# One stream over sequences, layers and groups in a fused scan, attention and feed-forward kernel

## The chip, the cores and the metric

The kernel runs on one core of a Trainium2 chip. The metric is the device time of one execution in microseconds; for each version the median of its runs is given. A profile is one further execution under the hardware profiler; its span is about 2 us shorter than the time of that execution.

## The reference

The input `x` is 32 sequences of 256 tokens with 256 features, float32. A first part is a small state-space model; two layers of local attention and feed-forward follow; the input is added at the end.

```
# scan part, per sequence
xr, gate = split(x @ W_in.T);  xr += cond
xc = silu(causal_conv4(xr));   xn = layernorm(xc)
B, C, dt = split(xn @ W_xproj.T);  dt = 0.01*tanh(dt @ W_dt.T + b_dt)
h = clip(h * (1 + dt*A) + B*min(|xn|,1) * xn[t], -10, 10)   # 256 steps, 16 states x 512
y = (C . h + D*xn) * silu(gate) @ W_out.T
# two layers, x = y
q, k, v = split(shift(x) @ wqkv);  q, k = l2norm, scale, rotary
x = x + local_attention(q, k, v, window 128, 8 heads of 64) @ wo
a, g = split(layernorm(shift(x)) @ w1 + b1)                  # 2 x 682
x = x + (a * gelu(g)) @ w2 + b2
# out = input + x
```

`shift` moves half of the features on by one token.

## The kernel before, in words

The sequences form four groups of eight (`NG = 4`, `GB = 8`). The program is recorded once; the order in which the recording calls are made sets, apart from small moves, the order of the instructions on each engine.

**Setup.** All constants are loaded on the ScalarE queue and prepared ahead of everything: the folded weights `wx_sb`, `wsum`, `wbias`, the rotary tables, the head tables. One flag, `bounded`, decides by a branch between two forms of the softmax; everything below is inside the branch that runs.

**Scan.** `group_scan` treats a group's eight sequences together in 8 chunks of 32 tokens. It keeps an agenda: each piece of work has a slot, slot t being the one in which step t is done. A chunk is prepared 43 to 4 slots before its first step: `project` (PE), convolution (DVE, GpSimd, ScalarE), norm, a transposition through DRAM. Each step is one custom VectorE instruction (`step`, L576) on a row `xrep` that was spread over the states by a DMA (512 KB for two rows, three buffers) and scaled by ScalarE (`scale_row`, L569). In the first group half of the rows are spread by TensorE instead (`by_tensor`). Read-out (`y`, L588), gate and output projection follow; the last piece is in slot 271. Result: `ys` in DRAM.

**Layers.** The group's residual is kept in SBUF in four tiles `res0` to `res3` of two sequences. In `Attention`, `project` makes q, k and v of half a sequence (L786) and rotates q and k on DVE and GpSimd; `turn` transposes them (L825); `scores`, `sums`, `values`, `divide` and `finish` (L836) do the rest. In `FeedForward`, two sequences go together: `normalise`, `spread`, then six chunks of `widen` (L1116, 512 columns), a Gelu and a product, and `narrow` (L1145), which adds up in two PSUM banks over all six. All PSUM tiles come from one pool of eight banks.

**Order.** The scan of group 0 runs alone. Then for each group `blocks` yields slot by slot: eight sequences of attention, eight slots each, then feed-forward of four pairs, and the same for layer 1. `side_by_side` lets the scan of the next group advance in even shares of its 316 pieces beside these slots, and ends it before the last pair. So attention and feed-forward are phases of a layer; each scan starts only when the last one has ended; the last group runs with no scan beside it. Weights of a layer come in four loads (`wqkv`, `wo`, `w1`, `w2`), each into one buffer.

Of the kernel before, what the change touches and what calls it, by code (L numbers as in the profile page):

```python
# [73 lines left out]
def kernel(  # L74
# [46 lines left out]

    w_in_sb = loaded(w_inT, [P, KM, 2 * DI], "w_in_sb", nc.sync)
# [5 lines left out]
    dskip_sb = loaded(d_skip.partition_broadcast(P), [P, DI], "dskip_sb")  # L128
    w_out_sb = loaded(w_outT, [P, NC_, DM], "w_out_sb")
    flg_sb = loaded(f_ln_g, [P, L, KM], "flg_sb")  # L130
    flb_sb = loaded(f_ln_b, [P, L, KM], "flb_sb")
    b1_sb = loaded(b1, [P, L, 2, len(MCH)], "b1_sb")
    b2_sb = loaded(b2, [P, L, KM], "b2_sb")
# [34 lines left out]
    nc.scalar.activation(a_sb, a_sb, AF.Tanh)  # L168
    nc.vector.tensor_scalar(a_sb, a_sb, -1.0, 0.01, ALU.mult, ALU.mult)


    nc.vector.tensor_scalar(w_out_sb, w_out_sb, 0.5, None, ALU.mult)


# [20 lines left out]
    for h in range(HEADS):  # L195
        row = 32 * (h // 2) + 16 * (h % 2)
        nc.vector.tensor_copy(
            head_rows[:, h, :], ident[:, row : row + 1].broadcast_to([P, DH])
        )

    b1g_sb = const.tile([P, L], FP, tag="b1g_sb", name="b1g_sb")
    nc.scalar.dma_start(
        out=b1g_sb[DH : DH + MREM], in_=b1[0:MREM, :, 1, len(MCH) - 1]
    )

    bounded = const.tile([1, 1], I32, tag="bounded", name="bounded")

# [8 lines left out]
    with tc.tile_pool(name="setup", bufs=2) as setup, tc.tile_pool(  # L216
        name="setup_ps", bufs=2, space=PSUM
    ) as sps:

        for src, pos, dst in ((qk_scale, rot_c, rc_sb), (qk_scale_sw, rot_s, rs_sb)):  # L220
            tab = setup.tile([P, NW, 2, DH], FP, tag="tab", name="tab")
            nc.scalar.dma_start(out=tab, in_=pos)
            for l in range(L):
                sc = setup.tile([P, 2 * DH], FP, tag="qk_sc", name="qk_sc")
                nc.scalar.dma_start(
                    out=sc, in_=src[l].rearrange("a d -> (a d)").partition_broadcast(P)
                )
                for w in range(NW):
                    nc.vector.tensor_mul(
                        dst[:, l, w].rearrange("p a d -> p (a d)"),  # L230
                        tab[:, w].rearrange("p a d -> p (a d)"),
                        sc,
                    )

        sq = setup.tile([1, L, 2, DH], FP, tag="sq", name="sq")
        nc.scalar.dma_start(out=sq, in_=qk_scale.unsqueeze(0))
        nc.vector.tensor_mul(sq, sq, sq)
        big = setup.tile([1, L, 2], FP, tag="big", name="big")
        nc.vector.tensor_reduce(big, sq, AX.X, ALU.max)
        nc.vector.tensor_mul(big[:, :, 0], big[:, :, 0], big[:, :, 1])  # L240
        nc.vector.tensor_scalar(big[:, :, 1], big[:, :, 0], SCALES2, None, ALU.is_le)
        allb = setup.tile([1, 1], FP, tag="allb", name="allb")
        nc.vector.tensor_reduce(allb, big[:, :, 1], AX.X, ALU.min)
        nc.vector.tensor_copy(bounded, allb)

        wx0 = setup.tile([P, NC_, 3 * NS], FP, tag="wx0", name="wx0")
        nc.scalar.dma_start(out=wx0, in_=w_xT)
        wdt_sb = setup.tile([NS, NS], FP, tag="wdt", name="wdt_sb")
        nc.scalar.dma_start(out=wdt_sb, in_=w_dtT)
        gcol = setup.tile([P, NC_], FP, tag="gcol", name="gcol")  # L250
        nc.scalar.dma_start(out=gcol, in_=s_ln_g.rearrange("(c p) -> p c", p=P))

        cols = setup.tile([P, NC_, 2], FP, tag="cols", name="cols")
        nc.gpsimd.memset(cols[:, :, 0:1], 1.0)
        nc.scalar.dma_start(out=cols[:, :, 1], in_=s_ln_b.rearrange("(c p) -> p c", p=P))
        for c in range(NC_):
            td = sps.tile([P, P], FP, tag="td", name="td")
            nc.tensor.transpose(td[0:NS, :], wx0[:, c, 2 * NS : 3 * NS], ident)
            wdT = setup.tile([NS, P], FP, tag="wdT", name="wdT")
            nc.vector.tensor_copy(wdT, td[0:NS, :])  # L260
            td2 = sps.tile([P, P], FP, tag="td", name="td2")
            nc.tensor.matmul(td2[:, 0:NS], wdT, wdt_sb, start=True, stop=True)
            nc.vector.tensor_copy(wx0[:, c, 2 * NS : 3 * NS], td2[:, 0:NS])
        nc.gpsimd.memset(wx_sb, 0.0)
        nc.vector.tensor_mul(wx_sb[:, :, 0 : 3 * NS], wx0, bc(gcol, 2, 3 * NS))
        for i in range(3):
            for src, k, dst in ((wx_sb, 0, wsum), (wx0, 1, wbias)):
                wide = setup.tile([P, NC_, NS, GB], FP, tag="wide", name="wide")
                nc.vector.tensor_copy(wide, bc(src[:, :, i * NS : (i + 1) * NS], 3, GB))
                tw = sps.tile([P, 2], FP, tag="tw", name="tw")  # L270
                for c in range(NC_):
                    nc.tensor.matmul(
                        tw,
                        wide[:, c].rearrange("p n b -> p (n b)"),
                        cols[:, c, :],
                        start=(c == 0),
                        stop=(c == NC_ - 1),
                    )
                nc.vector.tensor_copy(dst[:, i : i + 1], tw[:, k : k + 1])
        nc.vector.tensor_add(wbias[:, 2:3], wbias[:, 2:3], bdt_sb)  # L280
# [9 lines left out]
    def program(ctx, exact):  # L290
# [13 lines left out]

        def reorder(out, ps):

            nc.scalar.copy(
                out.rearrange("p (q i b) -> p b i q", q=NQ, b=GB),
                ps.rearrange("p (b i q) -> p b i q", q=NQ, b=GB),
            )  # L310

        def group_scan(g, ys):
# [9 lines left out]
            agenda = {}  # L322
# [3 lines left out]
            def at(s, what, *args):  # L326
                agenda.setdefault(s, []).append(partial(what, *args))
# [357 lines left out]
            def put_y(c, d):  # L685
                nc.scalar.dma_start(
                    out=ys[:, d, :, c * CH : (c + 1) * CH], in_=ck[c].pop(("yo", d))
                )

            def start():  # L690
                h0 = hp.tile([P, DI], FP, tag="h", name="h0")
                nc.vector.memset(h0, 0.0)
                state["h"] = h0

# [10 lines left out]
            if alone:  # L705
                at(-30, spread_weights)
            for c in range(NCH):
                for t in range(CH):
                    at(c * CH + t, step, c, t)
            for c in range(NCH):  # L710
                s0 = c * CH

# [27 lines left out]
                for d in range(KM):  # L740
                    at(s0 + 44 + 2 * d, copy_y, c, d)
                    at(s0 + 45 + 2 * d, put_y, c, d)
            for c in range(NCH):
# [23 lines left out]
            for s in range(min(agenda), max(agenda) + 1):  # L767
                for what in agenda.get(s, ()):
                    what()
                yield  # L770

        SCAN_PIECES = NCH * CH + 44 + 16

        def load_res(ys, j):
            t = rpool.tile([P, KM, 2, 1 + S], FP, tag=f"res{j}", name=f"res{j}")
            nc.gpsimd.memset(t[:, :, :, 0:1], 0.0)
            for k in range(KM):
                nc.sync.dma_start(out=t[:, k, :, 1:], in_=ys[:, k, 2 * j : 2 * j + 2, :])
            return t

        def project_qkv(l, res, wqkv_sb, b, w, a):
            ps = bank(ps_w, "w", "ps_qkv")
            for k in range(KM):
# [4 lines left out]
                    res[b // 2][:, k, b % 2, t0 : t0 + W],  # L788
                    wqkv_sb[:, k, a * DI : (a + 1) * DI],
# [42 lines left out]
        def project_out(res, wo_sb, b, oT):  # L832
            po = ps_w.tile([P, KM, S], FP, tag="w", name="ps_wo")
            for d in range(KM):
                for c in range(NC_):
                    nc.tensor.matmul(  # L836
                        po[:, d],
                        wo_sb[:, c, d * P : (d + 1) * P],
# [4 lines left out]
            rv = res[b // 2][:, :, b % 2, 1:]  # L843
# [15 lines left out]
        def attention(l, res, wqkv_sb, wo_sb):  # L859

            for b in range(GB):

                qTs, kTs, vs = [], [], []
                for w in range(NW):
                    for a in (2, 0, 1):
                        ps = project_qkv(l, res, wqkv_sb, b, w, a)
# [14 lines left out]
                oT = ap_.tile([P, NC_, S], FP, tag="oT", name="oT")  # L881
# [66 lines left out]
                project_out(res, wo_sb, b, oT)  # L948
                yield

        class Attention:
# [3 lines left out]
            def __init__(self, l, res, wqkv_sb, wo_sb):  # L955
                self.l, self.res, self.wqkv, self.wo = l, res, wqkv_sb, wo_sb
                self.qkv, self.rot, self.p, self.o = {}, {}, {}, {}

            def project(self, b, w, a):
                if w == 0 and a == 2:  # L960
                    self.qkv[b] = [
                        ap_.tile([P, HEADS // 2, S], FP, tag=n, name=n) for n in ("qT", "kT")
                    ] + [ap_.tile([P, NW, DI], FP, tag="v", name="v_sb")]
                ps = project_qkv(self.l, self.res, self.wqkv, b, w, a)
# [56 lines left out]
            def values(self, b):  # L1021
                oT = ap_.tile([P, NC_, S], FP, tag="oT", name="oT")
# [34 lines left out]
        class FeedForward:  # L1057
# [80 lines left out]
            def narrow(self, j, m):  # L1138
# [13 lines left out]
                if m < len(MCH) - 1:  # L1152
                    return
# [287 lines left out]
```

## Time and profile before

Three runs: 4162.62 us in the median (4139.63 to 4162.65). The profiled run has a span of 4150.5 us at a mean granted TensorE clock of 0.959.

| engine | busy us | share of the span | instructions |
|---|---|---|---|
| PE (matmul) | 3797.3 | 91% | 18236 |
| PEld (weight load) | 2008.9 | 48% | 18236 |
| DVE | 2627.6 | 63% | 4986 |
| ACT | 1810.9 | 44% | 3345 |
| POOL | 1699.9 | 41% | 1749 |

A float32 matmul shows as two records. Matmuls are pipelined and the end of a record is modelled, so PE counts as busy while it waits a little; periods between starts tell more. The timeline gives these landmarks: the first projection of the scan at 37.3 us, the first step at 69.6 us, the first projection of q, k and v at 478 us, the last step of the last scan at 3364 us, the end at 4150 us. The group of DVE steps is 894.7 us for 1024 steps (874 ns each), the scaling of rows on ScalarE 609.4 us for 896, with 702.6 us of idle time before them that ended with the DMA of the row.

### The profile page before, as it was taken

Reading aid. Unit: us, or ns where it says so; the run is one execution under the profiler, and the core shown is the slowest. Engines: PE = TensorE matmul, PEld = TensorE weight load, DVE = VectorE, ACT = ScalarE, POOL = GpSimd, SP = SyncE. Lnnn points to the kernel's source line nnn. Section 1 sums busy time; section 2 is a strip of 40 time slices with the busy share of each in tenths; the row PEclk is TensorE's granted clock in tenths of the full one; section 3 lists DMA queues with packets and bytes.
Section 4 is the critical chain, followed back from the end, with each engine's and each line's share of the span. In section 5 each row is a group of like instructions: output and inputs, shape, how many; then the busy total and the mean of one; then the engine's idle time right before and its main releaser. Section 6 shows DMA issues by size and latency. Waiting matters only on the chain. (4 is left out here: it accounts for less than half of the span.)

```text
span 4150.5 us, 51929 instructions
## 1 busy us (share of the span) xinstructions
PE 3797.3 (91%) x18236; PEld 2008.9 (48%) x18236; DVE 2627.6 (63%) x4986; ACT 1810.9 (44%) x3345; POOL 1699.9 (41%) x1749
## 2 busy tenths in 40 slices
PE   5898898899989999899898999889998899999999
PEld 3333355544555455444455445554455545654653
DVE  5888567777766456767767636777776744434433
ACT  2655344545445334444544424454544533323331
POOL 3333265325543166423654136532554316513531
PEclk8988899999999999999999999999999999999999
DMA  4444312444335312444433421244433421000000
GB/s 118 123 113 113 80 44 72 128 120 119 92 84 146 81 44 76 114 111 120 106 88 113 124 65 44 75 127 119 119 90 91 139 77 37 8 14 22 1 11 32
DMA packets 257346, 353.10 MB, mean 85 GB/s; under 512 B 160867, under 2 KB 170420, under 8 KB 254900
## 3 DMA queue, kind: packets, MB, share of 16 engines
q1 hardware_dynamic: 172624, 337.67, 29.8%
q10 hardware_dynamic: 84452, 12.01, 1.9%
q8 instruction: 147, 2.41, 0.3%
q14 instruction: 123, 1.01, 0.1%
HBM read 314.49 MB, written 33.55 MB: 84 GB/s over the span
## 5 line engine op out<-in xcount | busy, mean ns | idle before, releaser
L576 DVE CUSTOM_DVE_ANT_0 h<-h,xrep,lim 128x512 f32<-128x512 f32 x1024 | 894.7, 874 | 82.5 <-PE y L588 23.3
L569 ACT ACTIVATE xrep<-xrep,beta 128x512 f32<-128x512 f32 x896 | 609.4, 716 | 771.2 <-DMA xrep<-xnd 702.6
L786 PE MATMUL ps_qkv<-wqkv_sb,res 128*128 128x512 f32 x1536 | 750.2, 628 | 32.5 <-ACT oT L1036 8.2
L810 POOL TENSOR_TENSOR rot<-rot,swp 128x512 f32<-128x512 f32 x256 | 327.4, 1279 | 655.1 <-DVE swp L807 597.8
L786 PEld LDWEIGHTS ps_qkv<-wqkv_sb,res 128*128 128x128 f32 x1536 | 290.5, 199 | 386.9 <-issue 304.9
L818 POOL TENSOR_TENSOR rn<-ss,neg_half 128x8 f32<-128x8 f32 x256 | 436.7, 1706 | 23.3 <-DVE ss L816 11.7
L802 DVE TENSOR_TENSOR rot<-ps_qkv,rc_sb 128x512 f32<-128x512 f32 x256 | 175.7, 686 | 393.3 <-ACT sq L799 392.9
L1145 PE MATMUL po_f<-ag,w_sb 128*128 128x512 f32 (+1 forms) x768 | 358.9, 618 | 21.6 <-DVE ag L1126 21.5
L588 PE MATMUL y<-h,ly 128*32 128x512 f32 x2048 | 362.0, 631 | 14.3 <-DVE h L576 13.1
L1116 PE MATMUL pa<-hT,w_sb 128*128 128x512 f32 (+1 forms) x896 | 364.0, 597 | 0.0
L1126 DVE SCALAR_TENSOR_TENSOR ag<-pa,b_sb,gl 128x512 f32<-128x512 f32 x192 | 143.5, 748 | 320.3 <-PE pa L1116 147.5
L1116 PE MATMUL pg<-hT,w_sb 128*128 128x512 f32 x640 | 309.8, 607 | 0.3 <-ACT gl L1124 0.3
L333 PE MATMUL ps_in<-xg,w_in_sb 128*128 128x256 f32 x1024 | 291.1, 414 | 12.8 <-issue 4.5
L819 POOL TENSOR_TENSOR rot<-rot,rn 128x512 f32<-128x512 f32 x256 | 280.1, 1094 | 19.0
L380 DVE SCALAR_TENSOR_TENSOR acc<-xr,wc_sb,acc 128x256 f32<-128x256 f32 x384 | 199.4, 523 | 111.1 <-POOL acc L369 108.5
L1079 POOL TENSOR_TENSOR rstd<-ve,neg_half 128x1 f32<-128x1 f32 x128 | 77.9, 609 | 467.3 <-DVE ve L1077 461.6
L333 PEld LDWEIGHTS ps_in<-xg,w_in_sb 128*128 128x128 f32 x1024 | 191.0, 201 | 156.0 <-issue 71.9
L1000 ACT ACTIVATE pT<-sc 128x512 f32<-128x512 f32 x384 | 206.1, 592 | 127.4 <-PE sc L991 114.0
L836 PE MATMUL ps_wo<-oT,wo_sb 128*128 128x256 f32 x1024 | 237.3, 385 | 0.0
L1145 PEld LDWEIGHTS po_f<-ag,w_sb 128*128 128x128 f32 (+1 forms) x768 | 135.4, 191 | 203.1 <-issue 133.5
L799 ACT ACTIVATE sq<-ps_qkv 128x512 f32<-128x512 f32 x256 | 148.1, 592 | 187.0 <-PE ps_qkv L786 141.5
L991 PE MATMUL sc<-qT,kT 64*128 64x128 f32 (+1 forms) x2048 | 227.1, 352 | 1.9 <-ACT kT L830 1.8
(152 smaller groups left out, 5615.2 us busy)
## 6 DMA issues: line engine op xcount, KB each, us to landing
xrep<-xnd SPq DMA_DIRECT2D x448, 512.0 KB
xnd<-xn SPq DMA_DIRECT2D x64, 256.0 KB
wqkv_sb<-in_wqkv_dram SPq DMA_DIRECT2D x8, 1536.0 KB
xd<-xnd SPq DMA_DIRECT2D x192, 64.0 KB
w_sb<-in_w_dram SPq DMA_DIRECT2D x8, 1364.0 KB
xg<-in_xT_dram SPq DMA_DIRECT2D x64, 128.0 KB
ys<-yo ACTq DMA_DIRECT2D x64, 128.0 KB
res<-ys SPq DMA_DIRECT2D x32, 256.0 KB
```

Source lines behind the costliest of these rows:

```text
L333: nc.tensor.matmul(ps, w_in_sb[:, k, ch * P : (ch + 1) * P], ck[c]["xg"][:, k], start=(k == 0), stop=(k == KM - 1),)
L569: nc.scalar.activation(bx, ck[c].pop(("bx", t), bx), AF.Copy, scale=ck[c]["beta"][:, t : t + 1])
L576: nc.vector._custom_dve(TENSOR_ADD_SAT, out=h_new, in0=state["h"], in1=bx, s0=ck[c]["lim"][:, 0, t : t + 1], s1=ck[c]["lim"][:, 1, t : t + 1],
L588: nc.tensor.matmul(ck[c]["y", hb][32 * q : 32 * q + 32, :], ly[hb % 2][:, 32 * t : 32 * t + 32], ck[c].pop(("h", hb * TB + t)), start=(i = ...
L786: nc.tensor.matmul(ps, res[b // 2][:, k, b % 2, t0 : t0 + W], wqkv_sb[:, k, a * DI : (a + 1) * DI], start=(k == 0), stop=(k == KM - 1),)
L810: nc.gpsimd.tensor_add(rot, rot, swp)
L818: nc.gpsimd.tensor_tensor(rn, ss, neg_half, ALU.pow)
L819: nc.gpsimd.tensor_mul(rot, rot, bc(rn, 2, DH))
L836: nc.tensor.matmul(po[:, d], wo_sb[:, c, d * P : (d + 1) * P], oT[:, c, :], start=(c == 0), stop=(c == NC_ - 1),)
L991: nc.tensor.matmul(banks[r][:, i, :], kT[rows, i0 + i, kw * W : (kw + 1) * W], qT[rows, i0 + i, kw * W :], start=False, stop=(i == n - 1),)
L1116: nc.tensor.matmul(ps[0:n, :], self.w1[:, k, half_ * HID + o : half_ * HID + o + n], self.h[j][:, k].rearrange("p b t -> p (b t)"), start= ...
L1145: nc.tensor.matmul(self.po[d], self.w2[r0 : r0 + n, m, d * P : (d + 1) * P], self.ag[m][r0 : r0 + n, :], start=(m == 0), stop=(m == len(MC ...
```

## The change

The layers become one stream of 64 sequences (4 groups x 2 layers x 8), each with eight slots (`ST = 8`). In the slots of sequence n stand the attention of n, the projections of n + 1, `divide`, `finish` and `normalise` of n - 1, `spread` and `widen` of n - 2, and `narrow` of n - 3, over layers and groups without a break. It is meant to give TensorE other work where one sequence's attention waits, and to spread the load of the other engines evenly. For it

- feed-forward handles one sequence at a time: 256 columns for 512, Gelu and its product in one tile `ag`, one PSUM bank for both halves of `widen` and one for `narrow`, which runs all six chunks in a row;
- the residual has a tile for each sequence, weights come in slices (three of `qkv`, six of `w1`), each fetched when the last reader of the old one is past;
- qT, kT and oT have one buffer each, not two;
- the scans of all groups share one agenda: group g + 1 starts 256 slots after group g, so its preparation and first steps run beside the end of the one before. `scan_to` paces it: to slot 273 before the layers, then evenly to slot 529 in the first 114 slots of the stream, then 256 scan slots for 128;
- `bounded` is worked out first, from one load, and the rest of the setup moves into the agenda of the first scan (`constants`), the tables onto GpSimd.

The work is the same. Core of the diff:

```diff
-        def blocks(g, at, nxt):
...
-                for b in range(GB):
-                    more = b + 1 < GB
-                    more and at.project(b + 1, 0, 2)
-                    at.turn(b, 1)
-                    yield
...
-                pieces = feed_forward(ff, last)
...
-            side_by_side(blocks(g, at, nxt), scan, n_main, SCAN_PIECES)
+        ST = 8
+        seqs = [(g, l, b) for g in range(NG) for l in range(L) for b in range(GB)]
...
+        def attend(n, at, b, nxt):
+            stage(n, 0, at.turn, b, 1)
+            stage(n, 3, at.scores, b, 0, 0, 2)
+            stage(n, 2, at.scores, b, 1, 0, HEADS // 2)
+            stage(n, 5, at.scores, b, 0, 2, 2)
+            stage(n, 7, at.sums, b)
+            stage(n, 7, at.values, b)
+            stage(n + 1, 2, at.divide, b)
+            stage(n + 1, 5, at.finish, b)
+            if nxt is not None:
+                for w in range(NW):
+                    for i, a in ((0, 2), (1, 0), (1, 1)):
+                        stage(n, 3 * w + i, nxt[0].project, nxt[1], w, a)
+                stage(n, 6, nxt[0].turn, nxt[1], 0)
+
+        def feed(n, g, l, b):
+            ff = FeedForward(g, l, b)
+            for w in range(NW):
+                stage(n + 1, 6 + w, ff.normalise, w)
+                stage(n + 2, w, ff.spread, w)
+            for m in range(NM):
+                stage(n + 2, 2 + m, ff.widen, m)
+            for d in range(KM):
+                stage(n + 3, d, ff.narrow, d)
...
+        DRAIN = 17
...
+        scan_to(S + DRAIN)
...
+        group, reload = ST * L * GB, ST * (L * GB - GB + 6) + 2
+        for t in range(max(stages) + 1):
+            for what in stages.get(t, ()):
+                what()
+            g, r = divmod(t + 1 + group - reload, group)
+            lo, hi = (g * S + S + DRAIN), ((g + 1) * S + S + DRAIN)
+            if t + 1 <= reload:
+                scan_to(s0 + (2 * S + DRAIN - s0) * (t + 1) // reload)
+            else:
+                scan_to(lo + (hi - lo) * r // group)
```

```diff
-                pa = bank(ps_w, "w", "pa")
-                    pg, b1g = bank(ps_w, "w", "pg"), b1_sb[0:n, l, 1, m : m + 1]
+                ps = bank(ps_w, "w", "pa")
+                pa = ps[0:n, 0:S]
+                    pg, b1g = ps[:, S:], b1_sb[:, l, 1, m : m + 1]
...
-                gl = aw.tile([P, 2 * S], FP, tag="pT", name="gl", bufs=6)
-                nc.scalar.activation(gl[0:n, :], pg[0:n, :], AF.Gelu, bias=b1g)
+                ag = aw.tile([P, S], FP, tag="ag", name="ag", bufs=7)
+                nc.scalar.activation(ag[0:n], pg, AF.Gelu, bias=b1g)
...
-                oT = ap_.tile([P, NC_, S], FP, tag="oT", name="oT")
+                oT = ap_.tile([P, NC_, S], FP, tag="oT", name="oT", bufs=1)
...
+    bounded = const.tile([1, 1], I32, tag="bounded", name="bounded")
+    with tc.tile_pool(name="setup", bufs=1) as setup:
+        sq = setup.tile([1, L, 2, DH], FP, tag="sq", name="sq")
+        nc.sync.dma_start(out=sq, in_=qk_scale.unsqueeze(0))
...
+        def constants(at):
...
+            at(-43, load_w)
+            at(-34, fold_1)
+            at(-32, fold_2)
...
+            at(-16, load_later)
+            at(14, halve)
+            at(30, load_tables)
```

## The prediction

> **What bounds the kernel now.** I read the page first: the busy row, then the row of forty slices, to see whether one engine carries the whole span.
>
> ```profile
> PE 3797.3 (91%) x18236; PEld 2008.9 (48%) x18236; DVE 2627.6 (63%) x4986; ACT 1810.9 (44%) x3345; POOL 1699.9 (41%) x1749
> ...
> PE   5898898899989999899898999889998899999999
> ```
>
> TensorE is the only candidate, and it is busy almost everywhere after the first slice. But the page warns that a busy PE need not be PE at its peak, so I looked for a stretch where it is at its peak. In the last group no scan runs beside the layers. Two kinds of lines of the chain of waits (start, length, what) give the price of dense work there:
>
> ```profile
> 3496.62 3.65 PE ps_wo L836 x16
> ...
> 3523.25 3.65 PE ps_wo L836 x16
> ...
> 3549.88 3.65 PE ps_wo L836 x16
> ...
> 3694.47 1.85 PE pa L1116 x8
> ...
> 3725.77 1.85 PE pa L1116 x8
> ```
>
> The reader is to see two periods: the attention of one sequence comes round every 26.63 us, the feed-forward of two sequences every 31.3 us. So one sequence of one layer costs 26.6 + 15.7 = 42.3 us of dense TensorE work, and 64 of them 2706 us. The scan of a group at the same prices: 256 projections in and 128 out at 0.216 us (the chain has "PE rb L1044 x8" at 1.73 us, 0.216 us for a record of 256 columns), 64 read-outs of 8 records at about 1.0 us (the timeline), 64 records of raw sums, 128 transposes at 0.11 us: 55 + 28 + 64 + 14 + 14 + 3 = 178 us.
>
> Then I cut group 2 into its four stages (attention and feed-forward of layer 0, of layer 1) with the table by stretch; columns are length, busy time of PE, PEld, DVE, ACT and POOL, granted clock, DMA share, GB/s:
>
> ```profile
> 1534.00:1778.00 244.00, 215.92 (x1330) 131.46 (x1327) 164.76 (x314) 120.22 (x226) 130.63 (x126) 0.95 0.33 88
> 1778.00:2040.00 262.00, 246.40 (x989) 120.86 (x989) 192.37 (x367) 126.90 (x232) 101.36 (x116) 0.97 0.45 116
> 2040.00:2306.00 266.00, 235.46 (x1417) 139.25 (x1416) 188.19 (x349) 128.37 (x244) 125.58 (x121) 0.94 0.40 104
> 2306.00:2521.00 215.00, 206.64 (x751) 98.65 (x751) 107.76 (x205) 75.73 (x135) 64.20 (x70) 0.98 0.28 77
> ```
>
> The four are 987 us; dense work is 16 x 42.3 + 178 = 854, so 133 us of a group, 13.5%, are gaps. Pricing the matmul records of each stretch back to back gives 200, 232, 213 and 197 us, so the yield is 0.82 and 0.80 in attention, 0.89 and 0.92 in feed-forward. The loss sits in attention, although DVE is at most 71% busy there. One example from the timeline of such a stage shows its form:
>
> ```profile
> 1148.73 1.33 ACT L569 ACTIVATE xrep<-xrep,beta 128x512 f32<-128x512 f32 x2 [7.00 <-DMA xrep<-xnd]
> 1149.97 0.56 ACT L830 COPY qT<-tr_qk 128x512 f32<-128x512 f32 x1
> 1150.43 0.58 ACT L830 COPY kT<-tr_qk 128x512 f32<-128x512 f32 x1
> 1150.58 2.18 PE L786 MATMUL ps_qkv<-wqkv_sb,res 128*128 128x512 f32 x3 [2.12 <-ACT qT L830]
> ```
>
> ScalarE stood 7.0 us for a row of the scan, the copy of qT queued behind it held a PSUM bank, and PE waited 2.1 us. PE has nothing else in its order at that point, since its neighbours are all attention.
>
> **What the Trainium skill says.** "TensorE: Matmul & The Clock Gate", [...] section "Architectural detail: the array is 16x 32x32" says that PE pulls weight loads ahead of running matmuls. The trace agrees: a record of 256 columns takes 216 ns in a row although its load takes 190 (page, L836 PEld 189.9 us for 1024). So halving the columns of the feed-forward need not cost time. "PSUM — Partial Sum Buffer", section "Engine vs sequencer instructions", calls the queues of ScalarE and VectorE strict FIFO; the 7.0 us above is that. "ScalarE: Activation LUTs", section "What ACT_TABLE_LOAD costs", gives 1283 ns and 2.66 us with a drain. The trace has the 1283, but the next activation follows it within 12 ns and no drain shows, so I take 1.3 us:
>
> ```profile
> L1124 ACT ACT_TABLE_LOAD x8 | 10.3, 1283 | 0.1
> L1000 ACT ACT_TABLE_LOAD x7 | 9.0, 1283 | 0.1
> ```
>
> **The change part by part.**
>
> 1. Setup. Before, the branch on `bounded` stood behind 20 loads on the ScalarE queue, and the first projection of the scan behind the fold of the weights on PE: it starts at 37.3 us, the first step at 69.6. After, `bounded` needs one load and eight small DVE operations, and the first projection waits for `w_in_sb` alone (w_out_sb, half as large, landed 8.4 us after its issue), so it can start near 12 us. The fold follows in free slots. Of 25 us I take 20, since the weights' 3.3 MB now load beside the first chunk. The tables, done on GpSimd during the first scan (38% busy), cost nothing.
>
> 2. First scan alone, 70 to 478 us (DVE 337 of 408 us, 83%, so DVE paces it at about 1.5 us a step). Its slots -43 to 273 now also carry slots -43 to 17 of group 1: 17 steps of 0.87 and two chunks of preparation at about 12 us, 39 us of DVE. Some 29 us of it fall into idle DVE of the drain (DVE is 55% busy from 416 to 520 us). +10 us here. What is done here leaves later: about 27 us of PE work. Layers start at 478 - 20 + 10 = 468.
>
> 3. Matmuls of the feed-forward. Widen: 4 matmuls of 256 columns for 4 of 512 on two sequences; narrow likewise; twice as many at half the price: 0. Fewer PSUM banks are held (one for pa and pg, po for two slots, not the whole pair).
>
> 4. The stream. A stage is an eighth of a sequence: attention of one beside feed-forward of the one two before it. Until its 370th of 534 steps about two scan slots ride along. Work of these, leaving out about 12 stages' worth for the fill: 358 x 42.3/8 = 1892, and 3 x 178 - 27 = 507: 2399 us. The remaining 154 stages' worth, 814 us, run without a scan. The question is the yield. A sequence now lasts some 57 us where attention with a scan took 40, with the same chain of attention inside, and in front of each of its waits stand independent matmuls of widen or narrow. A row of the scan is due every 3.4 us rather than every 2.7. I halve the loss per sequence in attention (40 - 33 = 7 us to 3.5) and add 1 for feed-forward: 53.4/(53.4 + 4.5) = 0.92. So 2608 us.
>
> 5. Table loads. Gelu and exp now alternate: the built program has 374 loads where 15 stood, 359 x 1.3 = 467 us of ScalarE, about 7.8 us a sequence. ScalarE per group: 451 us in the four stretches above, plus 16 x 7.8 = 125, plus 9 for halved gelus: 585 of about 920, 64%. So it is not the bound; behind a load stand the exp, the copies of q, k, v and the rows of the scan, and for those PE waits through PSUM. The exp has two to four stages until its sums, so I cost this at nothing beyond the yield above. Bounds: 0 and 467 us, if each were seen in full.
>
> 6. DVE: 653 us in the four stretches, plus 16 for halved shapes: 669 of 920, 73%, as in feed-forward of layer 0 now. Single buffers for qT, kT and oT: each rewriting stands after the last reader in PE's order (turn in slot 6 after scores in 5; values in 7 after finish in 5): 0. Weights are fetched in slices two or three slots ahead of use, some 20 us for half a megabyte: 0.
>
> 7. Without a scan, and the end: 814/0.955 = 852, and 10 us more for the last sequence, whose add, norm and widening follow each other with little beside them. 862.
>
> Sum: 468 + 2608 + 862 = 3938; with 2 us between span and time, and rounding, **3940 us**.
>
> **The rivals.**
> - A, PE nearly dense. For it: without a scan attention repeats at 26.63 us to the hundredth. Yield 0.96 and 0.97: 468 + 2499 + 850 = 3817. Against: rows of the scan still arrive by DMA through ScalarE.
> - B, the waits remain: the loads and busier DVE use up the slack, and the yield stays 0.865 as now. 468 + 2773 + 870 = 4111.
> - C, slower: PE's rigid order meets a late gelu or exp in nearly every stage, yield as in the worst attention stage (0.80 to 0.82) and the loads show without a scan too (0.90): 468 + 2926 + 914 = 4308. For it: all five engines share every stage, and one late ScalarE instruction holds all. Against: slots leave 6 us or more between nearly all makers and users.
>
> **How the numbers follow.** Main case 0.66, A 0.14, B 0.13, C 0.07. Faster by over 1% means below 4121: main, A and about half of B, 0.87; within 1% the rest of B, 0.06; slower C, 0.07. The range takes in A's time and most of the way to B: 3815 to 4085.
>
> **What would show it.** Right: first scan step near 50 us; layers from about 468; a sequence about every 57 us with a scan and 43 to 45 without; no stretch with a scan under a yield of 0.88; DVE near 73%, ScalarE near 64% there; PE's waits for ScalarE after a row's DMA shorter. Wrong: PE idle behind `ag` or `pT` in each stage, ScalarE over 80%, a first scan well over 410 us, or sequences at 61 us and more.

## The result, and the profile after

The changed kernel takes 4011.88 us in the median of four runs (4008.98 to 4016.7); beside it, on the same chip, the kernel before took 4152.01. The ratio is 0.9656, with a 95% interval of 0.9632 to 0.9681: 140 us less. Forecast were 3940 us (range 3815 to 4085), which is 212 us less than 4152.

The page of the changed kernel, the rows that answer to those of before, and the granted clock (PE is TensorE, PEld its weight loads, DVE VectorE, ACT ScalarE, POOL GpSimd):

```profile
PE 3794.7 (95%) x20540; PEld 2375.0 (59%) x20540; DVE 2634.7 (66%) x5241; ACT 2327.0 (58%) x3895; POOL 1758.9 (44%) x1784
...
PE   7888889999999899999999999999999999999999
...
PEclk8899989999999999999999999999999999999999
```

The busy time of TensorE is what it was (3797.3); its share rose because the span shrank. So the place to look is not the amount of work but the waits between. The landmarks: first projection of the scan at 10.5 us (37.3 before), first step 53.6 (69.6), first projection of q, k and v 491.2 (478.1), last scan step 3133.2 (3364.0), end 4007.

The table by stretch (length, busy time of PE, PEld, DVE, ACT, POOL, granted clock, DMA share, GB/s) of the changed kernel, from the start of the layers to the first output projection, then to the end of group 1's scan, then two whole groups with a scan, then 16 sequences without one:

```profile
491.00:590.00 99.00, 84.34 (x385) 42.67 (x386) 81.30 (x138) 49.52 (x92) 61.38 (x56) 0.90 0.50 132
590.00:1270.00 680.00, 645.04 (x3689) 417.54 (x3687) 501.41 (x993) 432.94 (x733) 316.84 (x322) 0.98 0.40 103
1270.00:3133.00 1863.00, 1783.19 (x9979) 1149.18 (x9982) 1289.90 (x2549) 1162.98 (x1931) 854.30 (x841) 0.98 0.40 102
3216.00:3908.00 692.00, 692.00 (x3938) 470.99 (x3937) 296.10 (x658) 351.15 (x544) 279.13 (x237) 1.00 0.07 19
```

The kernel before, over the same two groups (last step of group 1 to last step of group 3), and over its 16 sequences without a scan:

```profile
1396.00:3364.00 1968.00, 1805.99 (x8962) 978.98 (x8961) 1309.50 (x2466) 902.43 (x1673) 843.51 (x862) 0.96 0.37 97
...
3450.00:4142.00 692.00, 673.76 (x3330) 371.43 (x3328) 292.33 (x568) 219.26 (x396) 265.96 (x224) 0.99 0.05 16
```

Two things are to be seen. A group with a scan beside it fell from 1968/2 = 984 us to 1863/2 = 931.5. And without a scan some 16 sequences take 692 us in both kernels. The stretch of before leaves out the first of its projections, so a whole period is the cleaner measure. In the chain of waits of before, eight sequences come round in 347.7 us:

```profile
3496.62 3.65 PE ps_wo L836 x16
...
3844.27 3.65 PE ps_wo L836 x16
```

That is 43.5 us a sequence. In the changed kernel 43.2 us pass from one output projection to the next at the end. With nothing beside it, **the mixed stream is worth next to nothing over the phases** (0.5%). While a scan runs, the timeline of the changed kernel shows 62.8 and 55.6 us by turns (two sequences share one chunk of the scan):

```profile
2601.64 3.62 PE L943 MATMUL ps_wo<-oT,wo 128*128 128x256 f32 x16
2664.43 3.62 PE L943 MATMUL ps_wo<-oT,wo 128*128 128x256 f32 x16
2720.05 3.62 PE L943 MATMUL ps_wo<-oT,wo 128*128 128x256 f32 x16
...
3562.05 3.62 PE L943 MATMUL ps_wo<-oT,wo 128*128 128x256 f32 x16
3605.29 3.62 PE L943 MATMUL ps_wo<-oT,wo 128*128 128x256 f32 x16
```

So the gain is in what the scan costs beside the layers: (984 - 692)/256 = 1.14 us a step before, (931.5 - 692)/256 = 0.94 us after, where my dense price for its matmuls was 178/256 = 0.70.

The gain comes with fewer waits of TensorE. Summed from the table of waits over the two groups, they are 80.6 us a group before and 39.8 after. The largest before, and the largest that are left (total, times, longest, over both groups):

```profile
PE tp_hn L1094 <- DVE ve L1077: 26.2, 6, 8.0
PE sc L984 <- DVE swp L807: 22.4, 16, 2.8
PE po_f L1145 <- DVE ag L1126: 14.9, 7, 3.5
```

```profile
PE rs L1118 <- DVE hn L1189: 48.1, 15, 3.8
PE ov L1137 <- DVE ve L1185: 12.8, 13, 1.0
PE rs L1118 <- ACT qT L937: 7.1, 11, 1.3
```

### The profile page after: what moved, and what is told of

It reads as the page before. It is cut to its first block, busy times and chain, and to the rows that moved or that the text cites. A ratio compares the mean times of both kernels' runs of the same rounds, so it can differ in the third digit from the quotient of the medians.

```text
span 4007.1 us, 57108 instructions
## 1 busy us (share of the span) xinstructions
PE 3794.7 (95%) x20540; PEld 2375.0 (59%) x20540; DVE 2634.7 (66%) x5241; ACT 2327.0 (58%) x3895; POOL 1758.9 (44%) x1784
## 4 chain that ended last, share of the span: by engine, by line
PE 55%; DVE 8%; POOL 7%; ACT 6%; DMA 5%; issue 3%; ACTq 0%; SPq 0%; POOLq 0%; DVEq 0%
PE ps_qkv L893 11%; PE pa L1224 9%; PE po_f L1247 8%; DMA xrep<-xnd 5%; PE ov L1137 4%; PE sc L1099 3%; PE ps_wo L943 3%; PE y L662 3%; DVE h L650 2%; PE ps_in L407 2%; PE rb L1152 2%; PE rs L1118 2%; POOL rn L925 2%; PE tr_qk L932 2%; PE ps_out L740 1%
## 5 line engine op out<-in xcount | busy, mean ns | idle before, releaser
L650 DVE CUSTOM_DVE_ANT_0 h<-h,xrep,lim 128x512 f32<-128x512 f32 x1024 | 926.3, 905 | 87.1 <-ACT xrep L643 31.8
L643 ACT ACTIVATE xrep<-xrep,beta 128x512 f32<-128x512 f32 x896 | 613.6, 718 | 546.0 <-DMA xrep<-xnd 455.9
L893 PE MATMUL ps_qkv<-qkv,res 128*128 128x512 f32 x1536 | 709.8, 598 | 1.7 <-DMA res<-ys 1.5
L1224 PE MATMUL pa<-hT,w 128*128 128x256 f32 (+1 forms) x3072 | 692.5, 387 | 2.3 <-ACT xn L527 1.7
L1224 PEld LDWEIGHTS pa<-hT,w 128*128 128x128 f32 (+1 forms) x3072 | 498.2, 178 | 210.8 <-issue 68.4
L893 PEld LDWEIGHTS ps_qkv<-qkv,res 128*128 128x128 f32 x1536 | 277.3, 190 | 273.6 <-issue 244.9
L1235 DVE SCALAR_TENSOR_TENSOR ag<-pa,b_sb,ag 128x256 f32<-128x256 f32 (+1 forms) x448 | 212.5, 475 | 298.1 <-ACT ag L1232 296.1
L1247 PE MATMUL po_f<-ag,w 128*128 128x256 f32 (+1 forms) x1536 | 382.4, 390 | 2.0 <-DVE ve L1185 1.3
L1247 PEld LDWEIGHTS po_f<-ag,w 128*128 128x128 f32 (+1 forms) x1536 | 276.5, 189 | 112.2 <-issue 54.5
L926 POOL TENSOR_TENSOR rot<-rot,rn 128x512 f32<-128x512 f32 x256 | 291.4, 1138 | 19.7
L1108 ACT ACT_TABLE_LOAD x186 | 238.6, 1283 | 19.0 <-PE sc L1099 12.9
L1232 ACT ACT_TABLE_LOAD x187 | 239.9, 1283 | 6.4 <-issue 2.1
L943 PE MATMUL ps_wo<-oT,wo 128*128 128x256 f32 x1024 | 232.0, 380 | 0.0
```

Of the source, the lines that this page charges most:

```text
L643: nc.scalar.activation(bx, ck[c].pop(("bx", t), bx), AF.Copy, scale=ck[c]["beta"][:, t : t + 1])
L650: nc.vector._custom_dve(TENSOR_ADD_SAT, out=h_new, in0=state["h"], in1=bx, s0=ck[c]["lim"][:, 0, t : t + 1], s1=ck[c]["lim"][:, 1, t : t + 1],
L893: nc.tensor.matmul(ps, res[b][:, k, t0 : t0 + W], wt["qkv", a][:, k], start=(k == 0), stop=(k == KM - 1),)
L943: nc.tensor.matmul(po[:, d], wt["wo", 0][:, c, d * P : (d + 1) * P], oT[:, c, :], start=(c == 0), stop=(c == NC_ - 1),)
L1108: nc.scalar.activation(p, banks[r], AF.Exp)
L1224: nc.tensor.matmul(pg if x else pa, wt["w1", m][:, k, x], self.h[:, k], start=(k == 0), stop=(k == KM - 1),)
```

## The experiments

I measured each kernel by its ratio to the kernel before on the same chip, and by two figures from its trace: the time of a group (last step of group 1 to last step of group 3, halved) and the waits of TensorE in it. Each kernel has one profile. Three more kernels below have the same stream as the changed one in these two groups (old setup, no scan in the first stages, convolution moved). They took 931.2, 921.6 and 929.6 us a group, so differences of 10 us and less say little. The two groups with their clock:

| kernel | ratio, 95% interval | group us | PE waits us a group | clock there |
|---|---|---|---|---|
| before | 1 | 984.1 | 80.6 | 0.96 |
| scans without gap alone | 1.0037, 1.0029 to 1.0045 | 974.5 | 72.2 | 0.96 |
| changed, with gaps | 0.9901, 0.9884 to 0.9919 | 964.0 | 57.3 | 0.97 |
| changed, in phases | 1.0306, 1.0289 to 1.0323 | 1026.0 | 101.7 | 0.95 |
| changed, bunched slots | 0.9887, 0.9867 to 0.9907 | 967.4 | 68.1 | 0.96 |
| changed | 0.9656, 0.9632 to 0.9681 | 931.5 | 39.8 | 0.98 |
| changed, no gelu | 0.9616, 0.9598 to 0.9634 | 911.7 | 24.9 | 0.99 |

**The changed kernel in phases.**

```diff
+        at_n = [16 * (n // GB) + n % GB for n in range(len(seqs))]
...
+            attend(n, ats[i], b, None)
+            if i:
+                lead(n, ats[i], b)
+            feed(n + GB - 2, g, l, b)
```

> All of the change is kept (setup, scans without a gap, finer pieces, buffers) but the feed-forward of a layer is put behind the attention of all eight sequences again, with eight pieces of stream for each, the scan spread evenly over twice as many stages. Theory M (the gain of the change is the mixing of attention and feed-forward, which lifts TensorE's yield beside a scan from 0.86 to 0.915): the yield falls back and the time is 4100 to 4170 us, although the table loads fall from 373 to some 30. Rival S (the gain is the setup, the closed gaps and the buffers): 4000 to 4040 us. Rival T (the table loads cost more than the mixing brings): under 3990 us.

4284.07 us, ratio 1.0306. It fell on the side of the mixing (theory M), but well outside its range, and is no clean test: it is 42 us a group worse than the kernel before, which is in phases too. Here a feed-forward has eight short stages with a scan slot in each. From its first to its last `pa`, a feed-forward phase with 59 to 66 steps took 209 to 223 us, where before one with 67 took 189 to 191. So the run mixes the cost of badly placed pieces with what mixing brings, and cannot tell them apart.

**The gaps put back.**

```diff
-                        slots.setdefault(i * S + s, []).extend(what)
+                        slots.setdefault(i * (S + 59) + s, []).extend(what)
...
-            lo, hi = (g * S + S + DRAIN), ((g + 1) * S + S + DRAIN)
+            SG = S + 59
+            lo, hi = (g * SG + S + DRAIN), ((g + 1) * SG + S + DRAIN)
```

> All of the change is kept but the scans of the groups follow each other at a distance of S + 59 slots again, so that the lead-in of one group begins when the slots of the one before have ended; the same number of stages carries 59 more slots for each group. Theory M: no work is added, so a gap costs the stream nothing, and as the alone scan of group 0 no longer carries the lead-in and first 17 steps of group 1, the layers start at 465 to 475 us instead of 491: 3985 to 4012 us in all. Rival S (closed gaps are part of the gain; 59 slots at the scan's 1.6 us a slot alone, for two or three gaps, come back in part): 4040 to 4120 us.

4115.18 us: theory M fell and rival S held. The layers did start at 471.1 us, 20 us earlier as expected, and all of it and 100 us more were lost in the stream. The table by stretch for the two groups:

```profile
1310.00:3238.00 1928.00, 1813.56 (x10057) 1173.30 (x10057) 1306.59 (x2597) 1155.48 (x1943) 842.00 (x863) 0.97 0.39 99
```

The busy times are those of the changed kernel within 2%, the time is 65 us longer. The starts of the output projections tell where: 56 to 72 us apart where 2.46 slots ride in a stage, 48 to 50 us in the gaps. The changed kernel has 2.0 slots in every stage and stays at 58.9 on average while the scan runs. A stage that carries more of the scan loses more than an empty one wins back.

**The gaps closed in the kernel before**, and nothing else:

```diff
...
-            side_by_side(blocks(g, at, nxt), scan, n_main, SCAN_PIECES)
...
+            lo, hi = done[0], (g + 2) * S + DRAIN
+            for i, _ in enumerate(blocks(g, at, nxt)):
+                if i + 1 <= n_main:
+                    scan_to(lo + (hi - lo) * (i + 1) // n_main)
+                else:
+                    scan_to(hi + S * (i + 1 - n_main) // n_all)
```

> The kernel before with one edit: its four scans run in one stream of slots, S slots apart, and go on beside the last feed-forward pieces of a group (attention and feed-forward stay in phases). The earlier runs gave what a scan step adds beside the stream (group time less 16 sequences of 43.2 us, over 256 steps): 1.12 us in the kernel before, 1.09 with mixing and gaps, 0.95 with mixing and no gaps. Theory E (what counts is how evenly the scan's slots are spread over the stages; the gaps alone are worth it with or without mixing): 1.00 to 1.05 us a step, layers 13 us later, 4080 to 4125 us. Rival I (closing the gaps pays only beside a mixed stream, as phases differ in what they leave free): 4140 to 4175 us. Rival G (closing the gaps is all of the gain): 4030 to 4065 us.

4165.31 us, rival I: no gain, in fact 0.4% more. So theory E fell, by which an even scan pays with or without mixing. A group is 10 us shorter, but the layers start 31 us later (508.9 us for 478.1), group 1's scan still ends 12 us later (1407.7 us for 1395.7), and 18 us more follow the last step.

```profile
1408.00:3357.00 1949.00, 1804.07 (x8902) 969.48 (x8901) 1291.12 (x2415) 896.74 (x1655) 814.92 (x835) 0.96 0.37 97
```

With this the two parts stand in a square: without mixing, closing the gaps changes the time by +0.4%; with mixing, it is worth 2.5 points (0.9901 to 0.9656). Mixing with gaps, which here includes the finer pieces and the buffers, is worth 1.0%, of which the setup (below) is 0.6. **Neither part does much alone; together they do nearly all.**

**Slots bunched within a sequence**, the direct test of evenness:

```diff
-                scan_to(lo + (hi - lo) * r // group)
+                q, p = divmod(r, 8)
+                scan_to(lo + (hi - lo) * (8 * q + min(2 * p, 8)) // group)
```

> The changed kernel, but after the first group each unit of eight stages takes its 16 scan slots in its first four stages (four a stage) and none in the other four, so the scan's rate over a sequence is the same and only its spread inside one is not. Theory E (what the change brings is that every stage carries the same small share of each engine's work, so fewer waits reach TensorE): visible waits of TensorE rise from some 47 us a group to 80 or more, its clock falls, and the time is 4040 to 4100 us. Rival U (it is enough that the scan runs beside some mixed stream all the time, as VectorE catches up within a sequence): 4000 to 4025 us.

4095.89 us, theory E, at the slow end of its range; the waits rose by less than I had said (68, not 80). Its two groups, and its largest waits of TensorE:

```profile
1271.00:3205.00 1934.00, 1797.59 (x9906) 1156.12 (x9899) 1269.98 (x2534) 1164.44 (x1919) 853.11 (x834) 0.96 0.37 98
```

```profile
PE tr_qk L932 <- ACT pT L1108: 66.1, 15, 5.7
PE ov L1137 <- DVE xd L711: 43.3, 12, 3.6
```

Every sequence has the same work and the same 16 steps, and nearly all take 61 to 64 us now. The ratio rose by 0.023, some 96 us: two thirds of the gain go when the same 16 slots stand in four stages of each eight. Rival U fell with this.

**No gelu.** The gelu becomes a tanh, so that ScalarE changes its table hardly ever.

```diff
-                nc.scalar.activation(ag[0:n], pg, AF.Gelu, bias=b1g)
+                nc.scalar.activation(ag[0:n], pg, AF.Tanh, bias=b1g)
```

> The gelu of the feed-forward is replaced by a tanh, which changes the function that the layer computes, so that nearly all of ScalarE's table loads (373 of 1.28 us, 479 us of its time) go and everything else stays. Theory M (ScalarE is not what ends the waits, and the loads fall into its idle time): 3975 to 4012 us. Rival T (the loads stand on the path: each delays the exp or gelu that TensorE waits for, a quarter of their time or more): under 3890 us.

4001.04 us, theory M in the sum: 0.4% below the changed kernel by the ratios (0.9616 for 0.9656), with intervals that just touch. But the stretches say it is less simple:

```profile
498.00:1305.00 807.00, 740.14 (x4071) 464.39 (x4071) 577.79 (x1132) 393.67 (x758) 378.64 (x379) 0.96 0.41 103
1305.00:3128.00 1823.00, 1773.14 (x9985) 1140.42 (x9987) 1291.10 (x2549) 904.48 (x1739) 838.47 (x841) 0.99 0.41 104
```

In the last two groups with a scan it saves 20 us each, of the (1163 - 904)/2 = 129 us that ScalarE has less to do. In the first, from the start of the layers to the end of group 1's scan, it takes 807 us for 779 in the changed kernel. The total hides these two, which nearly cancel. Why the first group loses is open.

**The old setup.** The constants are loaded and folded ahead of the branch again.

```diff
-                constants(at)
```

> All of the change is kept but the setup: the constants are loaded and folded ahead of the branch as in the kernel before, and the agenda of the first scan carries none of it. Theory M: the first step comes at 67 to 73 us instead of 53.6, the rest is unchanged: 4022 to 4035 us. Rival S (much of the gain lies in the setup): over 4060 us. Rival H (the setup was hidden behind the first projections in any case, and the pieces put into the agenda slow the alone scan by as much): 4000 to 4016 us.

4037.78 us, ratio 0.9713 (0.9696 to 0.9730), just above the range of theory M: the first step comes at 70.3 us and the layers at 512.4 instead of 491.2. The setup is worth 21 to 24 us.

**The first stages without a scan.**

```diff
-                scan_to(s0 + (2 * S + DRAIN - s0) * (t + 1) // reload)
+                scan_to(s0 + (2 * S + DRAIN - s0) * max(t + 1 - 12, 0) // (reload - 12))
```

> The changed kernel with the scan held still during the first 12 stages of the stream, and its slots put into the 102 stages after them (2.46 a stage instead of 2.20). Theory F (the first stages are slow, 99 us until the first output projection for some 63 us of TensorE work, because attention alone beside the scan loads VectorE to 82%): the first output projection comes at 545 to 560 us instead of 590; the denser stages after it give part back at 1.05 us a step, so 3990 to 4010 us in all. Rival E (spacing rules: what is saved at the start is lost later by the denser scan): 4012 to 4040 us.

4016.07 us, ratio 0.9671 (0.9653 to 0.9688), rival E. The first output projection came 73 us after the first projection of q, k and v, not 99; by the end of group 1's scan the kernel was 19 us behind the changed one. Spacing again: what the start won, the 2.46 slots a stage after it lost, and more. In the profile the two groups after that took 921.6 us each, for 931.5, and made up for it by the last step; as their stream is the same, this shows the scatter of one profile, or something carried over that no run here isolates.

**Feed-forward one stage later**, against the wait of `rs` shown above.

```diff
-                stage(n + 1, 6 + w, ff.normalise, w)
-                stage(n + 2, w, ff.spread, w)
+                stage(n + 1, 7 + w, ff.normalise, w)
+                stage(n + 2, 1 + w, ff.spread, w)
...
```

The timeline of the changed kernel shows the chain behind one such wait (start, length, instruction, and in brackets the idle time before it with what ended it):

```profile
1558.89 0.16 DVE L523 SCALAR_TENSOR_TENSOR stat<-mv,stat 128x1 f32<-128x1 f32 x1 [2.67 <-POOL stat L518]
```

```profile
1561.34 1.59 POOL L535 TENSOR_TENSOR xn<-xn,lnb_sb 128x512 f32<-128x512 f32 x1
1562.90 0.55 POOL L1187 TENSOR_TENSOR rstd<-ve,neg_half 128x1 f32<-128x1 f32 x1
```

```profile
1563.48 0.55 DVE L1189 TENSOR_SCALAR hn<-tp_h,mv,rstd 128x256 f32<-128x256 f32 x1 [1.39 <-POOL rstd L1187]
```

```profile
1564.18 1.58 PE L1118 MATMUL rs<-pT,head_cols 128*32 128x256 f32 x32 [3.71 <-DVE hn L1189]
```

The scan's norm holds up VectorE for 2.67 us and then GpSimd; the feed-forward's norm stands behind both, and its `tp_h` keeps a PSUM bank until 1564.03.

> The changed kernel with the feed-forward of each sequence put one stage later against the attention (normalise at stages 7 and 8 instead of 6 and 7, the rest likewise). In the changed kernel the only long waits of TensorE beside a scan are for the row sums of the softmax (26.3 us in 938 us, 8 times), which wait for a PSUM bank that the normalisation of the feed-forward one stage before still holds. Theory B (the bank is what they wait for): these waits go and nothing takes their place: 20 to 26 us a group, 3935 to 3965 us in all. Rival Q (VectorE's queue is late there, and whatever stands behind it waits as long): 4000 to 4025 us.

4012.45 us, ratio 0.9658 (0.9641 to 0.9675), rival Q. The waits of `rs` are gone and others stand in their place, 38.5 us a group for 39.8:

```profile
PE ps_st L559 <- DVE rhs L558: 28.2, 7, 4.3
PE tr_qk L932 <- ACT oT L1144: 21.9, 13, 2.5
```

The name in the table of waits was where the lateness of other engines reached TensorE, not where it came from.

**A fourth buffer for the broadcast rows.**

```diff
-        xp = ctx.enter_context(tc.tile_pool(name="xp", bufs=3, reuse_waits="tile"))
+        xp = ctx.enter_context(tc.tile_pool(name="xp", bufs=4, reuse_waits="tile"))
...
```

> The changed kernel with a fourth buffer for the scan's broadcast rows (the room comes from one buffer less for hT, ag, bcd and pi, which the order of the stages doesn't need). ScalarE waits 456 us in all for these rows, and exps and gelus stand behind the waiting scale. Theory D (an earlier load shortens the waits and with them TensorE's): 3960 to 3990 us. Rival N (the time of ScalarE isn't what the stream waits for, as with the table loads): 4000 to 4020 us.

4004.11 us, ratio 0.9643 (0.9625 to 0.9661), rival N: not to be told from the changed kernel. ScalarE's wait for these rows stayed at 456.8 us (455.9), so it is not the number of buffers that makes it.

**The convolution of the alone scan off VectorE**, three ways.

```diff
+                    if alone or (g == 1 and c == 0):
+                        nc.scalar.activation(
+                            cv, xr[:, :, k : k + CH], AF.Copy, scale=wc_sb[:, ch, k : k + 1]
+                        )
+                        nc.gpsimd.tensor_add(acc, acc, cv)
+                        continue
...
```

> The changed kernel with the convolution of the alone scan (and of the first chunk of group 1, prepared in it) taken off VectorE: ScalarE multiplies, GpSimd adds. Theory V (VectorE paces the scan until the layers start, 343 us busy of 397; the change let group 1's lead-in into these slots, which is why the layers started at 491 us and not at 468): 46 us leave VectorE, the layers start at 450 to 465 us, and the time is 3970 to 3990 us. Rival K (ScalarE, 229 us busy there and with 58 us more, or the longer chain over two engines holds the scan up instead): layers at 485 us or later, 4005 to 4030 us.

> The two edits that might help put together: the convolution of the alone scan off VectorE, and a fourth buffer for the broadcast rows, which by itself came out some 8 us below its neighbours. If both hold and add: 3960 to 3982 us. If the fourth buffer's 8 us are chance: the same as without it, within 4 us.

> The convolution of the alone scan off VectorE as before, but its first chunk left as it was, the last step of each channel two slots later, and buffers of its own for the products (one less for hT and ag). Without this spacing VectorE lost 34 us of work and 39 us went into waits for ScalarE's tanh at that step. Theory V (VectorE's work and the waits in its order are what paces the alone scan): first step at 54 us again, layers at 455 to 472 us, 3975 to 3998 us in all. Rival K (the alone scan is held by something else, the steps' own chain or the rows, at 1.55 to 1.6 us a slot): layers at 485 to 495 us, 4005 to 4020 us.

4015.64 us (0.9696, 0.9678 to 0.9713), 4011.66 us (0.9685, 0.9667 to 0.9703) and 4023.54 us (0.9675, 0.9659 to 0.9691): theory V fell each time, and the fourth buffer's 8 us did not come back. The layers start at 505.5 us with the convolution moved and at 514.0 with the spacing, later than even rival K had said for it (485 to 495). The alone scan in the changed kernel, and then with the spaced convolution:

```profile
53.00:450.00 397.00, 353.39 (x1311) 136.53 (x1310) 342.88 (x622) 228.71 (x424) 163.87 (x203) 0.91 0.45 115
```

```profile
53.00:450.00 397.00, 362.63 (x1250) 129.69 (x1249) 308.04 (x508) 266.55 (x521) 207.44 (x264) 0.93 0.42 109
```

VectorE fell from 343 to 308 us of 397, but in part because fewer steps fall into the stretch (237 for 249). Up to the start of step 256 it worked 335 us for 354, and yet that step came at 483.6 us for 461.6. TensorE, which spreads half of the rows in this stretch, is busy for 353 to 363 of the 397 us. No run here shows which of the two would have to be relieved, or both. No version that computes the same function beats the changed kernel by more than chance.

## Why the prediction was right, and where it was off

The side, the yield beside a scan and most terms held; the time came out 72 us, 1.8%, above the forecast, with two terms mis-sized that a third in part offset. Why the waits shrink was only half seen. By its steps:

- **Setup (step 1).** 20 us forecast; the first step came 16 us earlier, and putting the old setup back cost 21 us at the start of the layers. Right.
- **First scan alone (step 2).** +10 us forecast, since 29 of 39 us of VectorE work were to fall into idle time. Without group 1's slots the layers came at 471 us, with them at 491: 20 us showed, twice the term. Against 478 less 16 for the setup they came 29 us late; what makes the other 9 is open. From the first step to the layers it took 438 us, where well over 410 was to be a sign of being wrong. This term failed. Its reason, that VectorE alone paces this scan, is not borne out either: 19 us less of its work up to step 256 brought nothing.
- **Feed-forward matmuls (step 3).** Right: without a scan 43.5 and 43.2 us a sequence. In a dense row a record of 512 columns takes 429 ns, one of 256 takes 216.
- **The stream (step 4).** A sequence about every 57 us was forecast; the 43 that a scan rides beside throughout took 2532 us, 58.9 each, a yield of 53.4/58.9 = 0.907 for 0.92. The loss of a group at dense prices fell from 984 - 854 = 130 us to 931.5 - 854 = 77, where 16 x 4.5 = 72 had been forecast, and the visible waits halved, 39.8 us for 80.6. Mis-sized was the **fill**: I left 12 stages' worth of work out there and took 0.92 for what remains. It took 99 us for some 43 us of attention and 29 scan slots at 0.70, a yield of 0.64, 30 us more than at 0.92. Up to the 370th stage the stream took 2708 us (491 to about 3199), not 2608. By my estimate from these figures that is those 30, some 45 from the yield after it, and the rest work that I had put behind that stage.
- **Table loads (step 5).** Costed at nothing. Without 373 of them the time is 0.4% less, but that sums 20 us saved in each of the last two groups and 28 lost in the first. ScalarE is at 62% (64% forecast).
- **VectorE (step 6).** 69% in the two groups, 73% forecast; not the bound.
- **The end (step 7).** 862 us forecast, 808 measured: part of its work was done before stage 370, and the yield without a scan is 0.98, not 0.955.

The sum of these: +23 at the start, +100 in the stream, -54 at the end, 69 us between 3938 and the span of 4007.

The picture behind step 4 was too narrow. Its example was ScalarE held up by a row of the scan, and that wait did shrink (702.6 us of ScalarE's time before, 455.9 after). But of TensorE's 161 us of waits in the two groups before, 107 end with VectorE and 32 with ScalarE, and the largest single ones are in the feed-forward. I had also put independent matmuls of the feed-forward in front of the waits of attention, and costed the closed gaps only as a slower pace of rows. The runs show that the gain needs mixing and a scan without gaps together, and that the even spread of the slots carries most of it in the mixed stream: taking away either the closed gaps (0.9901) or the spread (0.9887) loses some two thirds of the gain. That mixing counts because it makes the stages alike fits these runs, also that even slots brought nothing in phases, but no run separates it from the independent matmuls that it puts in front of each wait.

I had also left out the clock. The Trainium skill, "TensorE: Matmul & The Clock Gate", section "HAM oscillation — how this bites in real kernels", says that TensorE's clock is throttled again after idle gaps of more than some 3.4 us, so that work after a gap starts slowly. The traces agree in kind, but shorter gaps were enough. One wait of the changed kernel, of 2.5 us, and what follows it (columns as above; the clock is the third figure from the end):

```profile
2255.00:2263.00 8.00, 8.00 (x52) 5.19 (x48) 6.76 (x10) 4.10 (x7) 6.70 (x6) 1.00 0.23 63
2263.00:2265.20 2.20, 0.00 (x1) 0.00 (x0) 0.78 (x4) 2.17 (x6) 1.75 (x2) 1.00 0.84 218
2265.20:2268.60 3.40, 3.12 (x34) 1.84 (x36) 2.19 (x8) 1.91 (x4) 0.54 (x1) 0.50 0.90 219
2268.60:2276.00 7.40, 7.40 (x59) 5.23 (x56) 4.09 (x7) 2.60 (x5) 0.46 (x1) 1.00 0.12 18
```

The same 32 matmuls of `rs` that took 1.58 us at 1564.18 (above) take 2.79 us here:

```profile
2265.48 2.79 PE L1118 MATMUL rs<-pT,head_cols 128*32 128x256 f32 x32 [2.48 <-DVE hn L1189]
```

In the two groups of the changed kernel 15 such stretches at half clock begin, each with 1.9 to 3.3 us of idle TensorE in the 3.4 us before it. In stretches of 50 us of before, changed, gaps and phases, the granted clock is 1.00 in the mean where TensorE stands under 0.3 us, 0.96 at 3 to 5 us, and 0.94 at 5 to 8 us (single ones 0.84 to 0.98).

So a wait costs more than its length. From before to changed the waits fell by 41 us a group and the group by 53. In the two groups, half clock was granted for 147 us before and for 72 after. Of that time TensorE stood idle for 26 and 10 us; half of the rest is lost, an estimated 30 us a group before and 15 after. The 41 us and this difference of 15 give 56, for the 53 measured. Between the other kernels of the table and the changed one, a microsecond of waits goes with 1.3 to 1.9 us of time. No run changed the clock alone.

## What to carry to other kernels

Where a side task runs beside a stream on engines with fixed order, spread it so that each short stage carries the same share; here the cost of a crowded stage was not paid back by an empty one. Mixing two kinds of work brought next to nothing by itself (43.5 and 43.2 us a sequence without a scan), and paid here only with an even side task beside it. A wait that is removed at the place where the table names it can come back elsewhere; follow it to the engine that is late first.

## What was not expected of the hardware

The granted clock fell to half after waits of as little as 2.5 us in an otherwise full TensorE. Its mean was 0.95 for the two groups of the kernel in phases (102 us of waits a group), 0.99 without gelu (25 us). A table load took 1283 ns throughout, and 373 of them (479 us of ScalarE) changed the time by only 0.4%:

```profile
L1108 ACT ACT_TABLE_LOAD x186 | 238.6, 1283 | 19.0 <-PE sc L1099 12.9
L1232 ACT ACT_TABLE_LOAD x187 | 239.9, 1283 | 6.4 <-issue 2.1
```
